# A second Strassen level for one of the seven half products of W2, with some evictions moved to ScalarE and new instruction lists

## The chip, the core and the metric

The kernel runs on one core of a Trainium2 chip, with one launch. The metric is the device time of that core in microseconds. Before the change it is 2509.16 us, the median of three runs (2508.62 to 2509.91). The engines are TensorE (PE in the profile; PEld is its loading of weights), VectorE (DVE), ScalarE (ACT), GpSimd (POOL) and SyncE (SP), which here only issues DMAs.

## What is computed

The input x is 128 graphs of 128 nodes with 256 features, in fp32; adj is 128 x 128. Four layers follow each other, each on h = max(layernorm(x), 0) and each added to x:

```python
# layer 0: gated sums over neighbours
x = x + relu((A_in h + eb) * sig(h g0) + (A_out h + oeb) * sig(h g1) + h * sig(h g2))
# layer 1: causal attention with adj as mask, weights Wqkv, Wo
x = x + softmax(q k^T / 16 + adj, causal) v @ Wo
# layer 2: three graph convolutions, weighting = adj * adj
h = relu(weighting (h W1)); h = relu(weighting (h W2)); x = x + weighting (h W3)
# layer 3: A_hat h, then Linear(256,512), batchnorm over all rows, relu, Linear(512,256), batchnorm
x = x + layer3(h)
```

W1 is 256 x 512, W2 512 x 1024, W3 1024 x 256. The batch statistics of layer 3 go over all 128 x 128 rows, so that layer is done in three passes: up to its first product, its second product, and the output.

## The kernel before

The 128 graphs are 32 groups (NG) of four; a group is T = 512 rows. The first pass takes a group through layers 0, 1 and 2 and the first product of layer 3, written z to DRAM. The change touches the first pass alone.

Big products are done by `seven` (L535), the Winograd form of Strassen's algorithm with one level: both operands are cut into quarters, and seven half-size products take the place of eight. Products 0, 5, 6 and 3 add up in one PSUM bank (px), 4 and 2 in another (pz), and product 1 has a bank of its own (py). In between ScalarE copies px or pz to a tile named kept (L542), and `put` lets VectorE add such a copy to a bank. The sums of quarters of the data are made by `sums` (L490 to L496), those of the weights once by `weight_sums` (L236).

`layer2` (L862) does W2 as two calls of `seven` (`wide(0)` and `wide(1)`; each takes 256 of the 512 columns of a half product), then W3. In `wide` each of the seven products is eight records of TensorE: 2 output chunks x 2 chunks of the contraction, 256 rows wide, each matmul leaving two records. The add of product 1 is at L885, and a relu by ScalarE follows (L887). `us` holds the quarters and sums of the activations u after mixing with the adjacency (uT).

`mixed` (L468) multiplies by an adjacency matrix: four 128 x 128 matmuls into one bank, then an eviction. The engines that evict are a tuple, used in turn; for uT (L857) and gT (L968) it held VectorE alone, for mT (layer 1) VectorE and ScalarE.

All these are Python generators that yield after each step. Which stream makes its next step is written out by hand in strings: HEAD for the first groups, TURN once for each of groups 1 to 29, and TAIL for the last two. In TURN a letter stands for a stream: A is layer 0 of group g + 2, B layer 1 of group g + 1 (b that of g + 2), C layer 2 of group g, D layer 3 of group g - 1 (d that of g). `in_turn` then ties the instructions of each engine, and DMA issues of POOL and SP, to this order, so that every engine works through its own queue in exactly the order of the letters.

Of the kernel before, what the change touches and what calls it, by code (L numbers as in the profile page):

```python
# [8 lines left out]
FP = mybir.dt.float32  # L9
AF = mybir.ActivationFunctionType  # L10
# [5 lines left out]
P = 128  # L16
# [6 lines left out]
def kernel(  # L23
# [58 lines left out]
    def bank(shape, name):  # L82
        return psum[-1].tile(shape, FP, tag="bank", name=name)
# [31 lines left out]
    ZT = {}  # L115

    weights = passA.enter_context(tc.tile_pool(name="weights", bufs=1))
    adj_sb = weights.tile([P, P], FP, name="adj_sb")
    nc.scalar.dma_start(adj_sb, adj)
    xin = passA.enter_context(tc.tile_pool(name="xin", bufs=4))  # L120
    X = {}
# [15 lines left out]
    gw = weights.tile([P, 3, D], FP, name="gw")  # L137
    gb = weights.tile([P, 3], FP, name="gb")
    nhalf = const.tile([P, 8], FP, name="nhalf")
    adjT = weights.tile([P, P], FP, name="adjT")  # L140
    ain = weights.tile([P, P], FP, name="ain")
    aout = weights.tile([P, P], FP, name="aout")
    maskb = weights.tile([P, P], FP, name="maskb")
# [7 lines left out]

    stats1 = weights.tile([P, FC, NG + 2, 6], FP, name="stats1")
    stats2 = const.tile([P, DC, NG + 1, 6], FP, name="stats2")
    bw1T_12 = weights.tile([P, F1 // 2], FP, name="bw1T_12")

    nc.gpsimd.memset(nhalf, -0.5)
    nc.gpsimd.memset(gb, 0.0)
# [34 lines left out]
    table = const.tile([P, 1], FP, name="table")  # L192
    nc.scalar.activation(table, nhalf[:, 0:1], AF.Exp)

    vrow = small.tile([NV, P], FP, name="vrow", bufs=1)
    deg = small.tile([P, 4], FP, name="deg", bufs=1)
    dinv = small.tile([P, 1], FP, name="dinv", bufs=1)

# [28 lines left out]
    def set_of(b, extra):  # L227
        b11, b21, b12, b22 = quarters(b)
        return b11, b21, b22, extra[:, 2], extra[:, 0], extra[:, 1], b12

    SETS = {}
    for k, b in ("2", w2), ("1", w1), ("3", w3), ("q", m_qk), ("v", w_vo), ("b", bw1T):
        _, nk, nf = b.shape
        SETS[k] = set_of(b, weights.tile([P, 3, nk // 2, nf // 2], FP, name=f"set_{k}"))

    def weight_sums(operands):  # L236

        b11, b21, b22, t4n, t1, t2, b12 = operands
        nc.vector.tensor_tensor(t1, b12, b11, ALU.subtract)
        yield  # L240
        nc.vector.tensor_tensor(t2, b22, t1, ALU.subtract)
        yield
        nc.vector.tensor_tensor(t4n, b21, t2, ALU.subtract)
        yield
        nc.vector.tensor_tensor(b12, b22, b12, ALU.subtract)
        yield

    BW2T = scratch.tile([P, FC, D], FP, name="BW2T")
    BW2S = scratch.tile([P, 3, FC // 2, D // 2], FP, name="BW2S")
    bw2s = bw1[:, :3, :].rearrange("p a (b c) -> p a b c", b=FC // 2)  # L250

# [13 lines left out]
    def warming():  # L265

        for n in FILL:
            awake(n)
            yield

    def gate_rows():

        for i, v in enumerate((gate_weight, out_gate_weight, loop_gate)):
            nc.sync.dma_start(
                gw[:, i, :], bass.AP(tensor=v.tensor, offset=v.offset, ap=[[0, P], [1, D]])
            )
        yield
# [76 lines left out]
    def last_weights():  # L354

        yield from turned(bw1T, bw1, FC, "bw1T")
        yield from turned(bw2t, bw2, DC, "bw2T")
        yield from weight_sums(set_of(bw2t, bw2s))
        nc.sync.dma_start(BW2S, bw2s)
        nc.sync.dma_start(BW2T, bw2t)  # L360
        yield
        pv = bank([P, NV], "pv")
        nc.tensor.transpose(pv, vrow, ident[:NV, :NV])
        yield
        nc.vector.tensor_copy(vecs, pv)
        yield
        nc.scalar.copy(bw1T_12, bw1T[:, 0, F1 // 2 :])
        yield
        yield from weight_sums(SETS["b"])

# [128 lines left out]
    def quarters_t(aT):  # L499

        return quarters(aT)
# [30 lines left out]

        return product

    def seven(product, put, shape, name, pool=None):  # L535

        def kept(pb, i):  # L540
            t = (pool or w).tile(shape, FP, tag="kept", name=f"{name}_t{i}", bufs=6)
            nc.scalar.copy(t, pb)  # L542
            return t

        px = bank(shape, f"{name}_x")
        product(0, px, True)
        yield SPLIT
        t1 = kept(px, 1)
        yield
        py = bank(shape, f"{name}_y")  # L550
        product(1, py, True)
        yield SPLIT
        yield from put((0, 0), py, t1)
        yield
        pz = bank(shape, f"{name}_z")
        product(4, pz, True)
        yield SPLIT
        t5 = kept(pz, 5)
        yield
        product(5, px, False)  # L560
        yield SPLIT
        t2 = kept(px, 2)
        yield
        product(2, pz, False)
        yield SPLIT
        yield from put((0, 1), pz, t2)
        yield
        product(6, px, False)
        yield SPLIT
        yield from put((1, 1), px, t5)  # L570
        yield
        product(3, px, False)
        yield SPLIT
        yield from put((1, 0), px, None)
        yield
# [105 lines left out]
    def layer1(g, bs=ALL):  # L681
# [172 lines left out]
        uT = tile_of(g, bs, [P, HC1, T], "uT", f"uT_{g}", 1)  # L854
        ex = tile_of(g, bs, [P, 3, HC1 // 2, T // 2], "us", f"us_{g}", 1)
        US[g] = summed(quarters_t(uT), ex)
        yield from mixed(uT, u, a2T, f"pmu_{tail}", (nc.vector.tensor_copy,), bs)  # L857
        if bs[-1] == G - 1:
            yield from sums(nc.vector, quarters_t(uT), ex)
        yield  # L860

    def layer2(g):  # L862

        us = US[g]
        h2T = w.tile([P, HC2, T], FP, tag="h2T", name=f"h2T_{g}", bufs=1)

        a11, a12, a21, a22 = quarters_t(h2T)
        ex = w.tile([P, 3, HC2 // 2, T // 2], FP, tag="h2s", name=f"h2s_{g}", bufs=1)
        h2s = (a11, a12, ex[:, 2], a22, ex[:, 0], ex[:, 1], a21)

        def wide(q):
            def put(ij, pb, other):
                i, j = ij
                j = j * HC2 // 2 + 2 * q
                dst = h2T[:, j : j + 2, i * T // 2 : (i + 1) * T // 2]
                if other is None:
                    nc.scalar.activation(dst, pb, AF.Relu)
                    mine = slice(2 * q, 2 * q + 2)
                    yield SPLIT
                    yield from sums(  # L880
                        nc.vector,
                        [a[:, mine] for a in (a11, a12, a21, a22)], ex[:, :, mine],
                    )
                else:
                    nc.vector.tensor_tensor(dst, pb, other, ALU.add)  # L885
                    yield SPLIT
                    nc.scalar.activation(dst, dst, AF.Relu)  # L887

            return seven(
                columns_by_half(us, SETS["2"], 2 * q), put, [P, 2, T // 2], f"p2_{g}_{q}"  # L890
            )

        S = []
# [57 lines left out]
    def layer3(g):  # L951
# [13 lines left out]
            yield  # L965
        gT = tile_of(g, parts[0], [P, DC, T], "dT", f"gT_{g}", 2)
        for i, bs in enumerate(parts):
            yield from mixed(gT, h, ahT, f"pg_{g}_{i}", (nc.vector.tensor_copy,), bs)  # L968
            if g < LAST:
                ex = w.tile([P, 3, 1, T // 2], FP, tag="ex", name=f"gs_{g}", bufs=2)  # L970
                gs = yield from sums(nc.vector, quarters_t(gT), ex)
            yield
# [29 lines left out]
        for i, j in (0, 0), (1, 0), (0, 1), (1, 1):  # L1002
            pb = bank([P, 2, T // 2], f"pz_{g}_{i}_{j}")
            for jj in range(2):
                for c in range(DC):
                    at = (2 * j + jj) * P
                    b = bw1T_12[:, jj * P : (jj + 1) * P] if (c, j) == (0, 1) else bw1T[:, c, at : at + P]
                    nc.tensor.matmul(
                        pb[:, jj, :], b, gT[:, c, i * T // 2 : (i + 1) * T // 2],
                        start=(jj == 0 and c == 0), stop=(c == DC - 1), skip_group_check=True,  # L1010
                    )
            yield from put((i, j), pb, None)
            yield

    def bn_part(stats, nch, groups, name):
# [7 lines left out]


    TURN = (
        "ACCCBCCCCCAADBDBBBCDDCDDCCDDABBBBBAADCCBBCBCDBBAADABDCBBABBCCCCCCAAACCCD"
        "CCCAADDDDAADCDDCCCDBBCCAADBBCDBBBBBBBBCCCCAAAAADDDBBbCCCCCCCbbBBBBBCCbbB"
        "BDDBBDBBBBBBBBCCBCCBBBCCCCBBBDBDDDDDDDBBBBBBBBbBBBBdbb"
    )
    BEGUN = 8  # L1030
    PINNED = tuple(
        getattr(mybir.EngineType, e) for e in ("PE", "DVE", "Activation", "Pool", "SP")
    )
    TAIL = (
        "CCCCCCCCCBBBBBDDDDDDBBBBBDDDCBBBCCCBBDDBBCCCBBCCCCCCBBCCCCCCCCCCCCBCDDBB"
        "BBBBBBBCCCBCCCCCCCCCBBBBBBBBBCCCBBBBDBBBBDDBDDDBCBCBBBBBCBDCCDDBBBBCCBBB"
        "BBBEBEEEEEEBBEEEEEEDDDFDEEEEEEFFFFFFFEEEEFDDEEEEDDDDEEEFFEEEEEDFDDEEEEDE"
        "EDEEEEEEESEEEEFEEFFEFFFEEFEEFGEFFGGFFFFFGFFFFGGGGGGGGGFFGFGGGGSE"
    )
    US, MIX = {}, {}  # L1040
    AHEAD = 3
# [14 lines left out]
    def part(f, g):  # L1056
# [4 lines left out]
    HALVES = range(G // 2), range(G // 2, G)  # L1061
    FILL = (5, 28, 6, 8, 9, 2, 4)
    HEAD = (
        "wiiwiaaaapppppcciiipmaaappwammaccccacaeeppppppccaccwaaceewaacapppppccbbw"
        "eeecppecwbbbbebddeeAembbbbbededdddbbbeeeogdbbbmbeedddbeooommdboooooobbbo"
        "bpdddemedbbbeddbedfffoobbbbbbpppdopdbbbbbbbbdCfffffdddfAAffnCCfffffffffA"
        "ddddfofpofoAddddndpAAfffddddddddfdffddCddfCCCCCCffnnACCCCfCoAACCACAACCCC"
        "CCCCCCCAAnnnnnAfCCCCCCoffffffAffffCCCCCCACCACCCCfffnCfAAAAABBBffffffffnC"
        "ConBfBffffoofCCCfCffffooCCfffCCCCCDDDffffffffffffBfBB"
    )  # L1070
    load_x(AHEAD)
    ds, bs = layer3(0), layer1(2)
# [2 lines left out]
        "b": layer1(0, HALVES[0]), "d": layer1(0, HALVES[1]),  # L1075
        "e": layer0(1), "f": layer1(1), "A": layer0(2), "B": bs, "C": layer2(0), "D": ds,
        "i": gate_weights(), "p": attention_weights(), "m": mixing_weights(), "n": network_weights(),
        "o": last_weights(), "w": warming(), "g": gate_rows(),
    }
    for k in HEAD:  # L1080
        at = len(nc.cur_bb.bb.instructions)
        next(stream[k], None)
        in_turn(at, PINNED)
    at = len(nc.cur_bb.bb.instructions)
    for k in "abcdefACipmnowg":
        for _ in stream[k]:
            pass
    assert len(nc.cur_bb.bb.instructions) == at
# [293 lines left out]
```

## Time and profile before

| | |
|---|---|
| median of three runs | 2509.16 us |
| the profiled execution | 2508.19 us |
| its span | 2506.4 us |
| granted TensorE clock | 0.997 |
| busy: PE / DVE / ACT / POOL | 2476.3 / 2006.6 / 1161.3 / 314.4 us |
| main loop, groups 1 to 29 | a turn of 68.73 us each |
| second pass and output | from about 2240 us on |

The profile is of one execution. Its lines of groups have the source line, engine, operation, output <- inputs by the names of tiles, shapes, and then busy time, mean duration in ns, and the idle time of the engine before them with what ended it. In the timeline the first number is the start in us from the span's start, the second the time from the first start to the last end of the merged instructions. Lines of waits have the sum in us, the number of times and the longest. Lines of a stretch have its length and then each engine's busy time in it.

### The profile page before, as it was taken

To read this page: it belongs to the slowest core of one execution; us is meant where nothing else is said; L and a number is where in the kernel's file an instruction comes from. 1 tells how busy PE (TensorE), PEld (TensorE's weight loads), DVE (VectorE), ACT (ScalarE), POOL (GpSimd) and SP (SyncE) were. 2 spreads that over 40 slices of the span, in tenths; PEclk is the share of its full clock that TensorE was granted. 3 is DMA by queue.
4 is the path that set the end of the run, shared out by engine and by line. 5 is a ranking of instruction groups with operands and counts; after the bars stand their busy time and mean duration, and the time that the engine had idled before them with its cause. 6 is when DMAs were issued, how large, how long until landed. Compare 5 with 4: busy or idle time off the path is not lost. (4 is left out here: it accounts for less than half of the span.)

```text
span 2506.4 us, 37984 instructions
## 1 busy us (share of the span) xinstructions
PE 2476.3 (99%) x13232; PEld 2189.2 (87%) x13232; DVE 2006.6 (80%) x4891; ACT 1161.3 (46%) x2486; POOL 314.4 (13%) x563
## 2 busy tenths in 40 slices
PE   9999999999999999999999999999999999999996
PEld 7888888888888888888888888888888888888885
DVE  7878887888888788887888887888878887568886
ACT  5344444444434444444444444444444444337767
POOL 2111111111111111110111111111101111000000
PEclk9999999999999999999999999999999999999998
DMA  4112222222222222222222222222222222145459
GB/s 153 43 51 76 73 79 85 85 76 76 76 79 82 64 72 77 76 84 85 78 74 78 83 77 64 74 79 72 85 85 80 76 72 76 26 158 210 170 198 388
DMA packets 136771, 237.83 MB, mean 95 GB/s; under 512 B 13938, under 2 KB 94852, under 8 KB 132612
## 3 DMA queue, kind: packets, MB, share of 16 engines
q1 hardware_dynamic: 130148, 212.79, 27.7%
q0 software_dynamic: 6288, 22.55, 2.5%
q8 instruction: 105, 1.72, 0.3%
q14 instruction: 86, 0.70, 0.1%
q10 hardware_dynamic: 144, 0.07, 0.0%
HBM read 120.93 MB, written 114.43 MB: 94 GB/s over the span
## 5 line engine op out<-in xcount | busy, mean ns | idle before, releaser
L423 ACT ACTIVATE h<-x,sh,rs 128x256 f32<-128x256 f32 x512 | 268.8, 590 | 109.6 <-POOL sh L409 99.4
L887 ACT ACTIVATE h2T<-h2T 128x512 f32<-128x512 f32 x192 | 120.8, 629 | 370.7 <-DVE h2T L885 370.7
L406 POOL TENSOR_SCALAR rs<-mv 128x4 f32<-128x4 f32 x124 | 36.1, 291 | 1751.9 <-DVE mv L402 1723.1
L527 PE MATMUL p_x<-uT,w 128*128 128x256 f32 x1024 | 242.2, 379 | 0.0
L527 PEld LDWEIGHTS p_x<-uT,w 128*128 128x128 f32 x1024 | 187.5, 190 | 22.3 <-issue 0.2
L398 DVE BATCH_NORM_STATS2 st<-x 128x6 f32<-128x256 f32 x512 | 187.0, 413 | 1.1
L542 ACT COPY p_t<-p_x 128x512 f32<-128x512 f32 (+1 forms) x192 | 97.3, 507 | 166.0 <-PE p_x L527 159.0
L605 DVE SCALAR_TENSOR_TENSOR gs<-h,gw 128x256 f32<-128x256 f32 x360 | 152.4, 423 | 15.1 <-ACT h L423 0.6
L407 POOL TENSOR_TENSOR rs<-rs,nhalf 128x4 f32<-128x4 f32 x124 | 142.2, 1147 | 10.3
L527 PE MATMUL p_x<-uT,set 128*128 128x256 f32 x512 | 121.1, 379 | 0.6 <-DVE h2T L885 0.6
L473 PEld LDWEIGHTS pmu<-a2T,u 128*128 128x128 f32 x1024 | 119.4, 192 | 2.1 <-PE pr L942 0.2
L527 PE MATMUL p_z<-us,w 128*128 128x256 f32 x512 | 121.1, 379 | 0.0
L527 PE MATMUL p_z<-us,set 128*128 128x256 f32 x512 | 121.0, 379 | 0.0
L527 PE MATMUL p_y<-uT,w 128*128 128x256 f32 x512 | 121.0, 379 | 0.0
L527 PE MATMUL p_x<-us,set 128*128 128x256 f32 x512 | 121.0, 379 | 0.0
L473 PE MATMUL pmu<-a2T,u 128*128 128x128 f32 x1024 | 119.7, 275 | 0.0
L527 PEld LDWEIGHTS p_z<-us,w 128*128 128x128 f32 x512 | 97.1, 190 | 25.2 <-issue 6.9
L836 ACT ACTIVATE u<-u 128x512 f32<-128x512 f32 x93 | 58.6, 630 | 127.0 <-DVE u L834 127.0
L917 PE MATMUL p_x<-h2T,w 128*128 128x256 f32 x480 | 113.4, 379 | 0.0
L994 DVE BATCH_NORM_STATS2 stats<-zo 128x6 f32<-128x512 f32 x120 | 77.3, 685 | 44.2 <-ACT zo L988 43.2
L527 PEld LDWEIGHTS p_x<-us,set 128*128 128x128 f32 x512 | 97.3, 190 | 13.2
L527 PEld LDWEIGHTS p_y<-uT,w 128*128 128x128 f32 x512 | 97.2, 190 | 13.2
(346 smaller groups left out, 5977.1 us busy)
## 6 DMA issues: line engine op xcount, KB each, us to landing
z<-zo SPq DMA_DIRECT2D x62, 512.0 KB, 5.3
zi<-z SPq DMA_DIRECT2D x31, 1024.0 KB, 4.9
x<-x POOLq DMA_DIRECT2D x32, 512.0 KB, 3.4
x<-in_x_dram SPq DMA_DIRECT2D x31, 512.0 KB, 3.8
hc<-h SPq DMA_DIRECT2D x120, 128.0 KB, 2.4
h<-hc SPq DMA_DIRECT2D x30, 512.0 KB, 3.5
sc<-s SPq DMA_DIRECT2D x120, 128.0 KB, 2.4
s<-sc SPq DMA_DIRECT2D x30, 512.0 KB, 4.2
```

Source lines behind the costliest of these rows:

```text
L398: nc.vector.bn_stats(st[:, k, :], xt[:, b, :])
L406: nc.gpsimd.tensor_scalar(rs, mv[:, :, 1], LN_EPS, None, ALU.add)
L407: nc.gpsimd.tensor_tensor(rs, rs, nhalf[:, :n], ALU.pow)
L423: nc.scalar.activation(dst, src, AF.Relu, bias=sh[:, k : k + 1], scale=rs[:, k : k + 1])
L473: nc.tensor.matmul(pm[:, k, :], src[:, b, c * P : (c + 1) * P], aT, start=True, stop=True)
L527: nc.tensor.matmul(pb[:, jj, :], b_r[r][:, c, at : at + P], a_r[r][:, c, :], start=(first and jj == 0 and c == 0), stop=(c == nk - 1), ski ...
L542: nc.scalar.copy(t, pb)
L605: nc.vector.scalar_tensor_tensor(gs, h[:, b, :], 1.0, gw[:, i, :], ALU.mult, ALU.mult, accum_out=gl[:, k, i : i + 1],)
L836: nc.scalar.activation(dst, dst, AF.Relu)
L887: nc.scalar.activation(dst, dst, AF.Relu)
L917: nc.tensor.matmul(pb, SETS["3"][r][:, c, :], h2s[r][:, c, :], start=(first and c == 0), stop=(c == HC2 // 2 - 1), skip_group_check=True,)
L994: nc.vector.bn_stats(stats1[:, 2 * j + jj, g, :], z[j][:, jj, :])
```

## The change

1. In `layer2`, for all groups but the first, product 1 of W2 (a12 by b21, 256 rows x 256 x 256 in each call) is no longer done as one product but by Strassen's algorithm again (`leaf`): seven products of 128 x 128 x 128, each one matmul. They alternate between two banks of their own (lx, ly), and VectorE adds the partial results onto the kept t1 or into h2T. `leaf_rows` makes four sums of quarters of a12 on VectorE, once for both calls. `leaf_sums` makes the weights' sums once, in HEAD (stream q).
2. The evictions of uT and gT alternate between VectorE and ScalarE.
3. The kept tiles have five buffers where they had six. The tile bw1T_12 is gone: its columns are written to DRAM in HEAD and read back on SP's queue into the tile of gs when layer 2 of the last group begins. adj_sb, adjT and vrow share the tiles of the leaf's weight sums.
4. HEAD, TURN and TAIL are new strings (TURN 222 letters for 198; the 24 more are all C).

```diff
-    def seven(product, put, shape, name, pool=None):
+    def seven(product, put, shape, name, pool=None, whole=True):
...
-            t = (pool or w).tile(shape, FP, tag="kept", name=f"{name}_t{i}", bufs=6)
+            t = (pool or w).tile(shape, FP, tag="kept", name=f"{name}_t{i}", bufs=5)
...
-        py = bank(shape, f"{name}_y")
-        product(1, py, True)
-        yield SPLIT
+        py = None
+        if whole:
+            py = bank(shape, f"{name}_y")
+            product(1, py, True)
+            yield SPLIT
         yield from put((0, 0), py, t1)
...
-        yield from mixed(uT, u, a2T, f"pmu_{tail}", (nc.vector.tensor_copy,), bs)
+        yield from mixed(uT, u, a2T, f"pmu_{tail}", (nc.vector.tensor_copy, nc.scalar.copy), bs)
...
+    def leaf_rows(a, extra):
+
+        a11, a12, a21, a22 = quarters_t(a)
+        s1, s2, s4, s3 = (e.rearrange("p (k t) -> p k t", k=1) for e in extra)
+        for out, one, two in (s1, a21, a22), (s2, s1, a11), (s4, a12, s2), (s3, a11, a21):
+            nc.vector.tensor_tensor(out, one, two, ALU.add if out is s1 else ALU.subtract)
+            yield SPLIT
+        return a11, a12, s4, a22, s1, s2, s3
+
+    def leaf(a_r, b_r, dst, t, name):
+
+        def product(pb, r, first):
+            nc.tensor.matmul(
+                pb, b_r[r][:, 0, :], a_r[r][:, 0, :], start=first, stop=True,
+                skip_group_check=True,
+            )
...
+        def onto(i, j, pb):
+            mine = part_ij(t, i, j)
+            nc.vector.tensor_tensor(mine, pb, mine, ALU.add)
+
+        def put(i, j, pb):
+            nc.vector.tensor_tensor(part_ij(dst, i, j), pb, part_ij(t, i, j), ALU.add)
+
+        px = bank([P, P], f"{name}_lx")
+        product(px, 0, True)
+        yield SPLIT
+        onto(0, 0, px)
+        yield SPLIT
+        py = bank([P, 2, P], f"{name}_ly")
+        product(py[:, 1], 4, True)
+        product(py[:, 0], 1, False)
+        yield SPLIT
+        onto(1, 1, py[:, 1])
+        yield SPLIT
+        product(px, 5, False)
+        yield SPLIT
+        onto(0, 1, px)
+        yield SPLIT
+        product(py[:, 1], 2, False)
+        yield SPLIT
+        nc.vector.tensor_tensor(dst[:, :, :P], py, t[:, :, :P], ALU.add)
+        yield SPLIT
+        product(px, 6, False)
+        yield SPLIT
+        put(1, 1, px)
+        yield SPLIT
+        product(px, 3, False)
+        yield SPLIT
+        put(1, 0, px)
+        yield SPLIT
...
+                if pb is None:
+                    if not leaf_a:
+                        spare = ex[:, 0, 2:, :].rearrange("p k (h t) -> p (k h) t", h=2)
+                        leaf_a.append(
+                            (yield from leaf_rows(us[1], [spare[:, k] for k in range(4)]))
+                        )
+                    yield from leaf(leaf_a[0], leaf_set(q), dst, other, f"p2_{g}_{q}")
+                    nc.scalar.activation(dst, dst, AF.Relu)
...
-                columns_by_half(us, SETS["2"], 2 * q), put, [P, 2, T // 2], f"p2_{g}_{q}"
+                columns_by_half(us, SETS["2"], 2 * q), put, [P, 2, T // 2], f"p2_{g}_{q}",
+                whole=(g == 0),
...
-            yield from mixed(gT, h, ahT, f"pg_{g}_{i}", (nc.vector.tensor_copy,), bs)
+            yield from mixed(gT, h, ahT, f"pg_{g}_{i}", (nc.vector.tensor_copy, nc.scalar.copy), bs)
```

Below, a product of the leaf is named by its number: l0 to l6; o00, o11 and o01 are its three adds onto t1 in the order of the code.

## The prediction, made before the changed kernel was run

> **What bounds the kernel now.** I read the page's busy shares and slices first, then one steady turn of the main loop as a stretch, then TensorE in order of time, then the waits.
>
> ```profile
> PE 2476.3 (99%) x13232; PEld 2189.2 (87%) x13232; DVE 2006.6 (80%) x4891; ACT 1161.3 (46%) x2486; POOL 314.4 (13%) x563
> PE   9999999999999999999999999999999999999996
> DVE  7878887888888788887888887888878887568886
> 1357.44:1426.17 68.73, 68.73 (x368) 60.99 (x367) 56.05 (x141) 30.24 (x67) 9.60 (x17) 1.00 0.28 77
> ```
>
> The last line is one turn (us, then busy PE, PEld, DVE, ACT, POOL, clock, DMA share). TensorE is busy for all of it; VectorE for 56.05 of 68.73 us (82%), ScalarE for 30.24. A busy PE need not run at its pace, so look at the starts:
>
> ```profile
> 1353.98 3.73 PE L473 MATMUL pmu<-a2T,u 128*128 128x128 f32 x32
> 1357.55 1.89 PE L527 MATMUL p_x<-uT,w 128*128 128x256 f32 x8
> 1359.28 1.89 PE L527 MATMUL p_y<-uT,w 128*128 128x256 f32 x8
> ...
> 1422.71 3.73 PE L473 MATMUL pmu<-a2T,u 128*128 128x128 f32 x32
> ```
>
> One matmul of the program leaves two records. 32 records of 128 columns take 1357.55 - 1353.98 = 3.57 us, **112 ns each**; eight of 256 take 1359.28 - 1357.55 = 1.73 us, **216 ns each**; two of 512 take 0.86 us in the timeline, 430 each. A turn issues 108, 254 and 4 of them (counted from the stages): 108 x 0.112 + 254 x 0.216 + 4 x 0.430 = 68.68 us. The turn from one pmu to the next is 1422.71 - 1353.98 = 68.73 us. So TensorE loses 0.05 us in a turn: pace, not waiting, sets the main loop. The one wait that costs is small:
>
> ```profile
> PEld py L805 <- issue: 7.4, 28, 0.3
> DVE s L912 <- PE p_z L917: 77.7, 28, 2.8
> ```
>
> (28 turns.) The py wait ends when VectorE's transpose of p lands; between the rows before and after it, about 0.13 us of TensorE are lost. VectorE on the other hand waits for TensorE, some 12 us in a turn.
>
> [...]
>
> ```profile
> L885 DVE TENSOR_TENSOR h2T<-p_y,p_t 128x512 f32<-128x512 f32 x64 | 43.7, 683 | 1.4 <-PE p_y L527 1.4
> L912 DVE TENSOR_TENSOR s<-p_y,p_t 128x256 f32<-128x256 f32 x32 | 13.5, 423 | 13.9 <-ACT p_t L542 13.7
> L243 DVE TENSOR_TENSOR set_v<-w_vo,set_v 128x128 f32<-128x128 f32 x1 | 0.3, 285 | 0.0
> L477 DVE COPY uT<-pmu 128x512 f32<-128x512 f32 (+1 forms) x132 | 79.7, 662 | 0.8 <-PE pmu L473 0.6
> ```
>
> **The change, part by part, for one group.**
>
> *TensorE.* The second half product of W2 (r = 1 in seven) is two times eight records of 256 columns: 16 x 0.216 = 3.46 us. In its place stand two times seven products of one matmul, 28 records of 128 columns: 28 x 0.112 = 3.14 us. Saved: **0.32 us**. It applies to groups 1 to 31 (whole stays for group 0): 31 x 0.32 = 9.9 us; with unrounded paces (111.6 ns, 216) 0.33 and 10.3 us. I take 10.3.
>
> *VectorE.* Away: two adds of 512 columns (2 x 0.683) and three evictions that go to ScalarE (two of uT, one of gT: 3 x 0.66): 3.35 us. New: four sums on a12, and in each half five adds of 128 columns and one of 256: 14 x 0.285 + 2 x 0.424 = 4.84 us. Net +1.5 us: 57.5 of 68.4 us, 84%. ScalarE gets 3 x 0.58 = 1.7 us: 32 of 68.4. Neither becomes a bound by its total. What hides the 1.5 us is VectorE's 12 us of waiting for TensorE, if the list puts it there.
>
> *The new waits.* A leaf's products return to the same two banks (px, py): product l5 needs the first add out of px, l2 the one out of py, l6 and l3 the next out of px. Behind a waiting product all of TensorE's queue stands. I laid the new TURN out letter by letter (A 24, B and b 79, C 81, D and d 38 steps: C has 24 more). Between l5 and its add's product lie 6 us of other matmuls in the first leaf; the tightest is l2 of the first leaf, whose add (o11) stands at the end of a long VectorE queue that begins at the previous turn's last pz adds. There are 24 VectorE instructions from the (1, 1) add of pz to o11. How long they take is read from the timeline:
>
> ```profile
> 1358.39 1.23 DVE L463 STREAM_TRANSPOSE hT<-h 128x1024 f32<-128x1024 f32 x1
> 1359.55 0.65 DVE L490 TENSOR_TENSOR us<-uT 128x512 f32<-128x512 f32 x1
> 1360.23 0.69 DVE L492 TENSOR_TENSOR us<-us,uT 128x512 f32<-128x512 f32 x1
> ...
> 1361.57 0.68 DVE L496 TENSOR_TENSOR uT<-uT 128x512 f32<-128x512 f32 x1
> 1362.17 1.24 DVE L463 STREAM_TRANSPOSE s<-s 128x1024 f32<-128x1024 f32 x1
> ```
>
> An instruction that doesn't depend on the one before starts about 0.07 us before that one's end (1359.55 against 1358.39 + 1.23 = 1359.62; 1362.17 against 1362.25). By these start-to-start times the 24 take 13.4 us, and they begin 0.2 us after their product's slot and hand over 0.1 us after their end: 13.7. TensorE has 5.3 us of matmuls to the turn's end and 8.7 in the next turn before l2: 14.0. So l2 is met with **0.3 us to spare**. In the same way l5 has 0.6, l6 0.3, l3 0.1; in the second leaf l5 0.5, l2 0.6, l6 0.6, l3 0.3. By whole durations, without overlap, the 24 would take 14.8 and l2 would be 1.0 us late. The trace shows the overlap in every turn, so I take no stall; 1.0 is kept as the upper end. A gain below nothing is excluded: no product can run ahead of TensorE's order.
>
> *Buffers.* kept goes from 6 to 5: by the layout at most four are alive at once (pz's t5 stays longest), so ScalarE's copies find one free. Cost zero; if not, a copy waits for a put, under 0.7 us of an engine that is idle half the time. Banks: p2 px, pqv px, pqv pz, pr1, lx, ly are the most at once, six of eight.
>
> *Head and tail.* leaf_sums: four VectorE adds of 256 columns once, 1.7 us, against some 3 us of evictions that leave VectorE there. One ScalarE copy goes; one 128 KB write and, in the last group, one 128 KB read on SP's queue come: the layout has tens of us between the read's issue and its use, and transfers of 128 KB land in 2.4 us by the page's DMA rows[...]. The new HEAD and TAIL are taken at zero, with 2 us either way: by stretches TensorE is idle for 4.0 of the first 66 us and 0.6 of the next 55, which a new order can shift. In the tail two leaf groups are among the 31. The output phase is unchanged.
>
> *Sum.* The profiled execution took 2508.2 us (span 2506.4), 1.0 under the median of 2509.16. 2508.2 - 10.3 = 2497.9 for it; against the median 2509.2 - 10.3 = **2499**.
>
> **The rivals.**
>
> *Slower: VectorE late at the leaf (0.10).* If the leaf's adds don't overlap (they are short, and two of four sums depend on the one before), l2 is 1.0 us late in each turn: 31 x (1.0 - 0.33) = +21, **2530**. It decides from 0.33 us of stall in a turn. For it: VectorE at 84%, slacks of 0.1 to 0.6 us. Against: VectorE's starts overlap in all rows that don't depend, and the list of before loses only 0.05 us at 82%.
>
> *Half given back (0.10).* Slacks of 0.1 and 0.3 us fail in part: one wait missed costs about what py's costs, 0.13; with one or two in a turn 0.2 is lost, 31 x 0.13 = 4 are gained: **2505**, half of it above the 0.2% mark.
>
> *Pairs don't keep 112 ns (0.07).* The gain is nil at 16 x 216 / 28 = 123 ns a record. pmu, pg and ps run in rows of eight and more; pairs of 128 between matmuls of 256 are in no row here (pqv has rows of four, which keep 110). At 120 the gain is 31 x 0.1 = 3: **2506**.
>
> *Head or tail gain (0.08).* The new lists take 3 us out of the head's losses as well: **2496**.
>
> **How the numbers follow.** The forecast, 0.65: 2497 to 2502. About 0.2% (5 us) can be told from no change here. Faster by more: 0.65 + 0.08 + half of 0.10 = 0.78. Within: 0.05 + 0.07 = 0.12. Slower: 0.10. The range goes from the head's gain, 2495, to the pairs' and half cases, 2507; it leaves out the slow rival and the edges.
>
> **What would show it.** Right: the turn from pmu to pmu at 68.4 us, 374 records, leaf records 112 ns apart, VectorE near 57.5 us in a turn. The slow rival would show as PEld waiting for the leaf's adds (l2, l3 first) and a turn over 68.7. Pairs at fault: starts over 120 ns apart with no wait named. Wrong in the lists: a head to the first steady turn that is longer or shorter by over 2 us.

## The result, and the profile after

The changed kernel takes **2500.62 us** (median of seven runs, 2499.95 to 2501.45). The kernel before, beside it on the same chip, takes 2508.74 us (2508.01 to 2509.91). The ratio is 0.9967, with a 95% interval of 0.9956 to 0.9979: 8.1 us less, where 10.3 were forecast. The profiled execution of the changed kernel took 2501.45 us, span 2499.6.

The page of the changed kernel, its busy shares and two rows of its slices:

```profile
PE 2469.3 (99%) x13604; PEld 2192.4 (88%) x13604; DVE 2021.5 (81%) x5230; ACT 1256.3 (50%) x2584; POOL 289.0 (12%) x563
...
PE   9999999999999999999999999999999999999996
...
DVE  7878888888888888888888888888888887568886
```

TensorE is still busy throughout, with 372 more records (12 in each of 31 groups). One turn as a stretch (columns as before: us; busy PE, PEld, DVE, ACT, POOL; clock, DMA share, GB/s):

```profile
1356.00:1424.50 68.50, 68.50 (x380) 61.05 (x379) 56.56 (x152) 33.34 (x70) 8.73 (x17) 1.00 0.27 78
```

VectorE and ScalarE have room left, 12 and 35 us. So the question is again how long a turn is. From pmu to pmu:

```profile
1348.63 3.73 PE L486 MATMUL pmu<-a2T,u 128*128 128x128 f32 x32
1352.20 1.89 PE L540 MATMUL p_x<-uT,w 128*128 128x256 f32 x8
...
1417.14 3.73 PE L486 MATMUL pmu<-a2T,u 128*128 128x128 f32 x32
```

1417.14 - 1348.63 = **68.51 us**; the first four turns of the loop have 68.46. What a turn takes without any gap between its records was measured further down: **68.60 us** with the old products (number 7) and **68.27** with the new ones (number 12). I call **lost** what a matmul starts later than the pace of the record before it (112, 216, 430 ns). The old turn of 68.73 lost 0.13, at py; the new one loses 0.19 and, from the fifth turn, 0.24. By place, py's loss is gone, and pu's and pg's have come. The waits of the changed kernel in the 28 turns from 188 to 2113 us (total us, times, longest):

```profile
PEld pqv_z L725 <- issue: 13.9, 58, 0.2
...
PEld pu_x L523 <- DVE u L849: 9.0, 28, 0.3
...
PEld pg L486 <- ACT h L436: 0.2, 1, 0.2
```

The first line costs nothing: weight loads that idle while matmuls still run (pqv_z starts at 1357.63, 1.72 us after pr's start at 1355.91: pr's four records of 430 ns). In the second one the load waits 0.32 us per turn, and TensorE loses 0.19 us there. It is none of the leaf's products: pu is W1's product, which the change doesn't touch. The timeline of the changed kernel at that place:

```profile
1344.99 1.03 PE L523 MATMUL pu_x<-w,mT 128*128 128x256 f32 x4
1345.85 1.03 PE L540 MATMUL pz_x<-gT,bw1T 128*128 128x256 f32 x4
1346.80 1.13 PE L523 MATMUL pu_x<-set,mT 128*128 128x256 f32 x4
1347.77 1.03 PE L540 MATMUL pz_x<-gT,set_b 128*128 128x256 f32 x4
```

```profile
1346.80 0.73 PEld L523 LDWEIGHTS pu_x<-set,mT 128*128 128x128 f32 x4 [0.32 <-DVE u L849]
```

```profile
1346.06 0.69 DVE L849 TENSOR_TENSOR u<-pu_x,pu_t 128x512 f32<-128x512 f32 x1
1346.92 0.69 DVE L1064 TENSOR_TENSOR zo<-pz_x,pz_t 128x512 f32<-128x512 f32 x1 [0.17 <-PE pz_x L540]
```

The second row of TensorE starts 0.86 us after the first, as paced; the third 0.95 after the second, and the fourth 0.97 after the third. Product 6 of `seven` goes into bank px, VectorE adds it up (put (1, 1)), and product 3 goes into the same bank, so it may not start before the add has read it. From the end of product 6's slot (1345.85) to the start of the add (1346.06) there are 0.21 us, the add takes 0.69, and the next product begins 0.05 after its end: a **round trip** of 0.95 in these rows. The record behind the one that waited also comes late, by 0.10 us (0.97 for 0.86, rounded): 1.05 in all. The load that waited begins at 1346.80 together with its matmul, while the load of the first row begins at 1344.78, 0.21 us ahead of its matmul; that this makes the 0.10 fits, but no run tests it. Only one product, 0.86 us, stands between. In the new TURN the last products are pu.r2, pu.r6, pz.r6, pu.r3, pz.r3 (r is the product's number).

In the kernel before, the same pair was covered. Its TensorE has W3's last product, 1.72 us, between pu.r6 (first row) and pu.r3 (third row), and nothing is lost there:

```profile
1349.66 1.03 PE L510 MATMUL pu_x<-w,mT 128*128 128x256 f32 x4
1350.53 1.89 PE L917 MATMUL p_x<-h2T,set 128*128 128x256 f32 x8
1352.25 1.03 PE L510 MATMUL pu_x<-set,mT 128*128 128x256 f32 x4
```

The new list took that product away from there and put one of half its length in its place.

### The profile page after: what moved, and what is told of

It is laid out like the page before. It is cut to its first block, busy times and chain, and to the rows that moved or that the text cites. A ratio compares the mean times of both kernels' runs of the same rounds, so it can differ in the third digit from the quotient of the medians.

```text
span 2499.6 us, 39001 instructions
## 1 busy us (share of the span) xinstructions
PE 2469.3 (99%) x13604; PEld 2192.4 (88%) x13604; DVE 2021.5 (81%) x5230; ACT 1256.3 (50%) x2584; POOL 289.0 (12%) x563
## 4 chain that ended last, share of the span: by engine, by line
PE 95%; ACT 2%; DVE 1%; issue 0%; POOL 0%; ACTq 0%; DVEq 0%; POOLq 0%
PE p_x L540 17%; PE p_z L540 9%; PE p_x L1001 8%; PE pmu L486 5%; PE pu_x L523 5%; PE po_x L1331 4%; PE pz_x L540 4%; PE p_z L1001 4%; PE pg L486 2%; PE pm L486 2%; PE po_z L1331 2%; PE py L820 2%; PE pr L1026 2%; PE p_lx L889 2%; PE pqv_x L730 2%; PE pm L684 2%
## 5 line engine op out<-in xcount | busy, mean ns | idle before, releaser
L411 DVE BATCH_NORM_STATS2 st<-x 128x6 f32<-128x256 f32 x512 | 179.4, 411 | 0.1
L420 POOL TENSOR_TENSOR rs<-rs,nhalf 128x4 f32<-128x4 f32 x124 | 136.0, 1097 | 10.3
L849 DVE TENSOR_TENSOR u<-pu_z,pu_t 128x512 f32<-128x512 f32 x31 | 21.4, 692 | 117.6 <-PE pu_z L523 117.6
L970 ACT ACTIVATE h2T<-h2T 128x512 f32<-128x512 f32 x130 | 78.2, 623 | 60.4 <-DVE h2T L968 60.4
L540 PEld LDWEIGHTS p_x<-uT,set 128*128 128x128 f32 x512 | 94.7, 190 | 11.8 <-DVE h2T L968 0.3
L1001 PEld LDWEIGHTS p_x<-h2T,w 128*128 128x128 f32 x480 | 91.1, 190 | 12.3
L540 PEld LDWEIGHTS p_z<-us,set 128*128 128x128 f32 x512 | 92.5, 190 | 10.1
```

The source lines that it names most:

```text
L411: nc.vector.bn_stats(st[:, k, :], xt[:, b, :])
L420: nc.gpsimd.tensor_tensor(rs, rs, nhalf[:, :n], ALU.pow)
L540: nc.tensor.matmul(pb[:, jj, :], b_r[r][:, c, at : at + P], a_r[r][:, c, :], start=(first and jj == 0 and c == 0), stop=(c == nk - 1), ski ...
L1001: nc.tensor.matmul(pb, SETS["3"][r][:, c, :], h2s[r][:, c, :], start=(first and c == 0), stop=(c == HC2 // 2 - 1), skip_group_check=True,)
```

## Experiments

A time in the text below is a median; the kernel before stood at 2508.6 to 2509.1 in every comparison. Losses per turn are read from starts, as above.

### Where the wait comes from

**1. W3's last product moved into the gap.** Two letters of TURN move behind pu.r6 (CC behind BBBBB), one d by one letter.

```diff
-"...bBbBBBDCBBBBBCCCBBBBBDDDCBBDD..." "dBBbBb"
+"...bBbBBBDCBBBBBCBBBBBCCDDDCBBDD..." "BdBbBb"
```

> The changed kernel with two letters of C (W3's product r3 and its copy) moved behind pu's product r6, so that 2.6 us of matmuls instead of 0.9 stand between pu.r6 and pu.r3; d goes one letter later, behind the second sum of us. Theory: the missing part of the gain is the wait of pu.r3 for its add, 0.19 us in each turn, and it comes from the place in the list alone. Then a turn goes from 68.51 to 68.3 us and the time to 2500.6 - 29 x 0.19 = 2495. Rival: the wait is VectorE's new load and turns up elsewhere, or the swap of s, now 1.7 us later, makes VectorE's transpose late: the turn stays at 68.5 and the time at 2500 to 2502.

Measured 2506.11 us, ratio 0.999 (0.9982 to 0.9998): 5.5 us slower than the changed kernel. The waits of this kernel:

```profile
PEld pz_x L540 <- DVE zo L1064: 9.0, 28, 0.3
PEld pu_z L523 <- ACT pu_t L555: 7.5, 28, 0.3
```

The old wait is gone, and the same one has come up at pz: pz.r6 and pz.r3 now have only pu.r3's 0.86 between them, and lose the same 0.187. pu.r2 follows its copy too closely (0.134), since W3's product no longer stands ahead of it. In six turns pr, which needs the later swap of s, loses up to 0.48 us besides, 1.7 us in all. The theory's time was wrong: a pair may not be mended alone. That the pair decides, and not VectorE's load, is still what fits: the loss is 0.187 at either place.

**2. Without the leaf.** All of the change stays but the leaf: product 1 is done as one product in every group, the leaf's other letters do nothing, and of its four weight sums the last, which overwrites a block of the weights, is left out.

```diff
-                if pb is None:
-                    if not leaf_a:
...
-                elif other is None:
+                if other is None:
...
-                whole=(g == 0),
+                whole=4 * (g > 0 and q == 0),
```

> The changed kernel with its lists and evictions, but with product 1 of W2 whole again, at the letter of the leaf's first product; its add stands at the letter of the leaf's add of two quarters, the other letters of the leaf issue nothing. Theory: the leaf saves 0.33 us a group and the wait of pu.r3 is not its doing, so it stays: 2500.6 + 31 x 0.33 = 2511, the turn 68.84, pu.r3 still waiting 0.19. Rival: the 1.5 us of VectorE's new work make that wait; without them it goes and the time is 2505. Second rival: the new lists brought the gain, and the time stays near 2501.

Measured 2513.80, ratio 1.002 (1.0011 to 1.0028). pu.r3 still loses 0.188 in each turn, so this wait belongs to the new list and not to the leaf. The turn is 68.90, 0.39 more than with the leaf: 0.33 by the pace, 0.10 by a wait of pqv_z that appears where the leaf's products stood, less 0.05 at pg. In these lists the leaf is worth 13 us, 10 of them by its own products. Its stretch also gives the leaf's load on VectorE:

```profile
1300.00:1368.90 68.90, 68.90 (x368) 60.99 (x367) 54.38 (x138) 33.16 (x70) 8.64 (x17) 1.00 0.26 77
```

**3. No cover at all.** pz.r6 and its add go behind pu.r3 (the DDD of TURN moves by three letters).

```diff
-"...CBBBBBCCCBBBBBDDDCBBDDBb..."
+"...CBBBBBCCCBBBBBCBBDDDDDBb..."
```

> The changed kernel with pz.r6 and its add behind pu.r3 instead of before it: nothing stands between pu.r6 and pu.r3. Theory: the whole round trip shows, about 1.05 us instead of 0.19 in each turn, 2500.6 + 29 x 0.86 = 2525. Rival: the wait is not of this pair but of VectorE's queue as a whole, which also has less ahead of it now: under 0.5 us a turn, below 2510.

Measured 2555.70, ratio 1.0184 (1.017 to 1.0198):

```profile
PEld pz_x L540 <- DVE zo L1064: 32.0, 27, 1.2
PEld pu_x L523 <- DVE u L849: 32.0, 27, 1.2
```

I had counted one pair, but pz.r6 and pz.r3 have become neighbours too. Each of the two loses **1.05 us** in every turn. So the round trip with nothing between is 1.05, and with 0.86 between it 1.05 - 0.86 = 0.19: the loss in the changed kernel, to the hundredth.

### Evictions on ScalarE

**4. The changed kernel with the evictions back on VectorE.**

```diff
-f"pmu_{tail}", (nc.vector.tensor_copy, nc.scalar.copy), bs)
+f"pmu_{tail}", (nc.vector.tensor_copy,), bs)
...
-f"pg_{g}_{i}", (nc.vector.tensor_copy, nc.scalar.copy), bs)
+f"pg_{g}_{i}", (nc.vector.tensor_copy,), bs)
```

> The changed kernel with all evictions of uT and gT on VectorE again, lists unchanged. Theory: the leaf's waits have 0.3 to 0.6 us to spare, and two more evictions (1.2 us) in VectorE's queue ahead of the leaf's adds use that up: l4, l5 or l2 are late by 0.6 to 0.9 us in a turn, 2500.6 + 31 x 0.75 = 2524. Rival: VectorE idles 12 us in a turn and absorbs 1.9 us: 2501 to 2503.

Measured 2525.39, ratio 1.0067 (1.0053 to 1.0081): 24.8 us more than with ScalarE's share. The turn is 69.35 or a little less, with 0.30 lost at pr, 0.20 to 0.36 at the leaf's l2, 0.18 at the leaf's products 4 and 1, and pu's 0.19. So VectorE late at the leaf, which the slow rival of the forecast feared, lies near, though here it comes from more work in the queue and not from adds that fail to overlap. What kept it away are three evictions per turn; how much of that is uT's and how much gT's was not tried in these lists.

**5. The kernel before with both evictions shared**, nothing else (the reverse of that diff).

> The kernel before with the evictions of uT and gT shared with ScalarE, lists unchanged. Theory: TensorE keeps its pace there with 0.05 us of loss in a turn, so relief of VectorE brings nothing: 2508 to 2509.5, the turn 68.7. Rival: the relief is a gain of its own: 2 us or more less.

Measured 2523.97, ratio 1.0061 (1.0045 to 1.0076). I had not expected 15 us more. py's loss rises from 0.13 to 0.65 per turn. Timelines of this kernel, of ScalarE and of VectorE:

```profile
1397.13 0.63 ACT L887 ACTIVATE h2T<-h2T 128x512 f32<-128x512 f32 x1 [1.18 <-DVE h2T L885]
1397.66 0.57 ACT L542 COPY p_t<-p_z 128x512 f32<-128x512 f32 x1
1398.13 0.91 ACT L643 ACTIVATE m<-eb,gt 128x256 f32<-128x256 f32 x2
1398.94 0.57 ACT L477 COPY gT<-pg 128x512 f32<-128x512 f32 x1
```

```profile
1399.54 0.42 DVE L490 TENSOR_TENSOR gs<-gT 128x256 f32<-128x256 f32 x1 [1.15 <-ACT gT L477]
...
1402.62 0.68 DVE L463 STREAM_TRANSPOSE p<-pT 128x512 f32<-128x512 f32 x1
```

gT's second product starts at 1393.34 (8 x 112 ns: through by 1394.3), but its copy begins at 1398.94. ScalarE is idle a good part of the time (in the kernel before it was busy for 30.24 of a turn's 68.73 us), and the copy still stands in it behind a relu that waits for VectorE, a copy and two bias copies. VectorE, which has to sum gT next, idles for 1.15 us, and the transposition of p, which py waits for, stands behind that.

**6. The same for uT alone.**

> The kernel before with only the evictions of uT shared with ScalarE, those of gT left on VectorE. Theory: the 15 us that both together cost come from gT's second eviction, which stands behind four copies of layer 0 in ScalarE's queue, so that VectorE waits 1.15 us for it and p's transpose and py are late; uT's alone costs nothing: 2508 to 2510. Rival: ScalarE is late for exp because of uT: 2515 or more.

Measured 2509.12, ratio 1.0002 (0.9994 to 1.001), py at 0.12: all of the 15 us come from gT's eviction, and uT's gives nothing here.

**7. Number 5 with gT's product and copy issued a few letters earlier**, ahead of that relu.

```diff
-"...BBCCCCCCAAACCCD" "CCCAADDDDAADCDD..."
+"...BBCCCCCCAAACDDC" "CCCCAADDDAADCDD..."
```

> before_scalar_evict with the second product of pg and its eviction on ScalarE issued a few letters earlier: on TensorE nothing changes place, on ScalarE the copy goes ahead of a relu of h2T, a copy of p_z and two bias copies (m<-eb). In before_scalar_evict pg's matmuls ended near 1394.5 us and the copy began at 1398.9, while the first sum of gT idled VectorE for 1.15 us. Theory (the 15 us are this place in ScalarE's queue and nothing else): the copy begins within 1.7 us of its product, VectorE's idle time there goes, the transposition of p is no later than before, py waits no more than before (0.13 us in a turn), and the time is the kernel before's, 2508.8 us, or up to 3.5 us less as VectorE has 2 us less to do in each turn. Rival (ScalarE's share as such costs, wherever it stands): py still waits 0.4 us or more, and the time stays above 2516 us.

Measured 2505.11, ratio 0.9985 (0.9978 to 0.9992). Timeline of ScalarE in this kernel (the matmuls of gT's second product begin at 1381.70 in it):

```profile
1384.21 0.56 ACT L477 COPY gT<-pg 128x512 f32<-128x512 f32 x1
```

py's loss is zero, the turn 68.60. The eviction's place in ScalarE's queue is worth 19 us (2523.97 - 2505.11). Well placed, the shared evictions gain 4 us without any leaf, which is py's loss, 0.13 x 29 = 3.8 us.

### Toward a version without losses

**8. Three places at once.** pz.r6 goes ahead of pu.r2, W3's last product behind pu.r6, the transposition of s (d) behind us.s4, pr0 and pr1 behind pqv's product 4.

```diff
-"CCCBCCCCBBBCDDDBBBCBCCC..." "...CBBBBBCCCBBBBBDDDCBBDDBb..." "dBBbBb"
+"CCCBCCCCBBBCBBDDDBCBCCC..." "...CBBBBBCDBDBBBBCBCCDDBDBb..." "BBdbBb"
```

> The changed kernel with TURN laid anew by hand at three places: pz.r6 moves ahead of pu.r2, W3's r3 behind pu.r6, so that at least 1.7 us of matmuls stand between each pair that shares a bank (pu r5 and r6, pu r6 and r3, pz r6 and r3); the transpose of s goes behind the third sum of us, and the two products pr behind pqv's r4, because the swap of s now starts 2.6 us later. Theory: what is missing of the gain is the round trip of about 1.05 us (0.2 to the add, 0.69 for it, 0.05 and a bare weight load back) against 0.86 of cover, so a turn goes from 68.51 to 68.3 us and the time to 2500.6 - 29 x 0.19 = 2495. Rival: the late swap takes it back at pr or in the leaf: 2500 or more.

Measured 2502.80, ratio 0.9977 (0.9968 to 0.9986). In most turns all three waits are gone (68.32, pg's 0.05 left). But the swap of s through DRAM starts 2.6 us later, and in several of the loop's first ten turns it comes too late; timeline of such a turn:

```profile
323.37 0.34 SPq L472 DMA_DIRECT2D s<-sc  x1
329.31 1.25 DVE L476 STREAM_TRANSPOSE s<-s 128x1024 f32<-128x1024 f32 x1 [1.98 <-DMA s<-sc]
330.61 0.70 PE L1026 MATMUL pr<-s,a2T 128*128 128x512 f32 x1 [1.50 <-DVE s L476]
```

The read is issued at 323.37, and VectorE waits for it until 329.31, 5.9 us after the issue; the median landing of this read is 4.1 in the DMA rows of the changed kernel. These turns lose up to 1.95 us at pr, 6.8 us in all, and the tail another 1.3: the rival, a late swap that takes the gain back, came true. Why the read lands late in these turns was not traced.

**9. The same, and layer 3's second pair of relus ahead of the W2 copy on ScalarE** (in TURN, "CCCCCABDBB" becomes "CCCCDCABBB").

> The same, and the second half of layer 3's relus goes ahead of one relu of h2T in ScalarE's queue, so that pg no longer waits for it (0.05 us a turn). Theory: 1.5 us under the run before, 2493.5. Rival: the relu of h2T, now 1 us later, makes the sums of h2s late, and nothing is gained.

Measured 2501.06, ratio 0.9968 (0.9956 to 0.9981). Steady turns are 68.27, and pg's wait is gone. The late swaps stay, 6.8 us in the first ten turns and 1.2 in the tail.

**10. The transposition of s taken into the next turn**, and the leaf's products 4, 1 and 5 ahead of pr0 and pr1; TAIL is laid in the same way. The diff is against number 9.

```diff
-"CCCBCCCCBBBCBBDDDBCBCCCBBCCCCBBC..." "BBdbBb"
+"CCCBCCCCBBCDBCCCCBBBBDDDBCCBCCBBC..." "BBBbBb"
...
-    ds = after(8, ds)
+    ds = after(9, ds)
```

> The order of both_covered_relu, and the start of the turn laid anew so that the swap of s has more time: the transposition of s goes from the end of one turn into the next (behind the leaf's first sum on VectorE), and its two products pr0 and pr1 stand behind the leaf's products 4, 1 and 5 and behind products 4 and 5 of q and v on TensorE, 1.55 us later than in both_covered (0.45 + 0.22 + 0.88). The tail is laid the same way. Theory (what both_covered_relu still lost, 6.1 us in turns 2 to 10 and 1.2 in the tail, was the late swap alone): pr waits at most 0.4 us in any turn, steady turns stay at 68.3, and the time is 2501.1 - 6.1 - 1.2 = 2493.8 us, with 2492.5 to 2496 taken as a hit. Rival (the start of the turn has no room for it): VectorE stands in its queue for pr1 ahead of q's first put, so the leaf's last products (p_lx of product 3, slack 0.1 us in my lay-out) or product 2 wait 0.2 to 0.5 us in every turn, the turn becomes 68.5 to 68.8, and the time is 2500 to 2508 us.

Measured 2545.49, ratio 1.0147 (1.0132 to 1.0163). The swap is never late, as the theory had it, but every turn takes 70.01; start of a turn on TensorE:

```profile
1311.97 0.61 PE L730 MATMUL pqv_y<-w_vo,hT 128*128 128x128 f32 x4
1313.29 0.46 PE L889 MATMUL p_ly<-h2s,leaf 128*128 128x128 f32 x2 [0.71 <-DVE h2s L882]
1313.59 0.39 PE L889 MATMUL p_ly<-uT,w 128*128 128x128 f32 x2
1314.47 0.49 PE L889 MATMUL p_lx<-h2s,leaf 128*128 128x128 f32 x2 [0.49 <-DVE p_t L899]
```

I had moved the leaf's product 4 ahead by 2.6 us (to 3.7 us after the turn's first product, from 6.3, counted without the loss) without asking when its operand is there: the first sum of the leaf stands in VectorE's queue behind the sums of uT and hT and ends at 1313.14 (0.95 lost). The first add out of lx stands behind the leaf's other sums (0.76). The rival had the leaf and VectorE's queue, but named other products (3 or 2) and pr1 as what stands ahead, and put the loss at 0.2 to 0.5 us where it is 1.7.

**11. The relus alone**, on the changed kernel: the edit of number 9 and nothing else.

> The changed kernel with one letter of the turn moved: the second pair of relus of layer 3 is issued ahead of the eviction of W2's wide product behind it on ScalarE. Theory (pg's wait for this relu, 0.05 us in each turn from turn 5 on, is the rest of the loss that the evictions on ScalarE brought): the wait goes and nothing else moves, 24 x 0.05 = 1.2 us, 2499.4 us, pu's wait of 0.19 stays. Rival: the eviction that is passed is itself met with little to spare, W2's next product waits for it, and the time is the changed kernel's 2500.6 or up to 2 us more.

Measured **2498.68**, ratio 0.996 (0.9948 to 0.9973), 68.46 in every turn, no wait at pg. Expected were 2499.4.

**12. Number 11 with product 6 ahead of product 2 in pu.** Its order is now 6, 2, 3; pz.r6 and its add (two letters D) stand between 6 and 2, and the relu of part (0, 1) follows that of (1, 0).

```diff
+        rest = ((2, pz, (0, 1), t2), (6, px, (1, 1), t5))
+        for r, pb, ij, t in rest[::-1] if six_first else rest:
+            product(r, pb, False)
+            yield SPLIT
+            yield from put(ij, pb, t)
+            yield
...
             if other is None:
                 nc.scalar.activation(dst, pb, AF.Relu)
+                nc.scalar.activation(late[0], late[0], AF.Relu)
...
-"...BBBBBCCCBBBBBDDDCBB..."
+"...BBBBBCCCBBBDDBBDCBB..."
```

> relu_first with the last products of u (pu) in the order 6, 2, 3 in place of 2, 6, 3, the last product of z (pz.r6) between 6 and 2, and the relu of put (0,1) behind the one of put (1,0) on ScalarE. So pz.r6 and pu.r2 (1.72 us) lie between pu.r6 and pu.r3, which overwrites the bank that VectorE's add reads, and pu.r2 and pu.r3 (1.72 us) lie between pz.r6 and pz.r3; W3's last product, and with it the swap of s, stays where it is. The round trip was 1.05 us. Theory (the 0.19 us of a turn is the pair with 0.86 us of cover, and nothing else is near): the wait goes, turn 68.46 - 0.19 = 68.27, time 2498.7 - 29 x 0.19 = 2493.2 us, with 2492 to 2495 taken as a hit. Rival (the wait turns up elsewhere, as with W3's product moved): pmu waits for the relus at the end of u, or the swap, or pu.r6 for ScalarE's copy, 0.1 to 0.2 us in a turn, and the time is 2496 to 2500 us.

Measured **2494.22** (2492.28 to 2494.88), ratio 0.9941 (0.9927 to 0.9954): 14.6 us under the kernel before and 6.4 under the changed one. The same place as above, on TensorE of this kernel:

```profile
1338.61 1.02 PE L523 MATMUL pu_x<-w,mT 128*128 128x256 f32 x4
1339.47 1.03 PE L540 MATMUL pz_x<-gT,bw1T 128*128 128x256 f32 x4
1340.33 1.03 PE L523 MATMUL pu_z<-w,ms 128*128 128x256 f32 x4
1341.20 1.03 PE L523 MATMUL pu_x<-set,mT 128*128 128x256 f32 x4
1342.06 1.03 PE L540 MATMUL pz_x<-gT,set_b 128*128 128x256 f32 x4
1342.92 0.27 PE L486 MATMUL pmu<-a2T,u 128*128 128x128 f32 x1
```

Every row starts 0.86 or 0.87 after the one before. Both pairs have two products between them, W3's product and the swap behind it stay where they were, and all turns of the loop take 68.27 us: nothing is lost any more.

## Why the forecast was right, and where it was not

**TensorE paces the loop, and a leaf saves 0.32 to 0.33 us.** Right. Turns without a gap take 68.60 and 68.27. The 0.05 us that TensorE was said to lose in a turn came from rounded paces, which sum to 68.68; against the 68.60 it is the 0.13 of py's wait. The forecast counted 374 records in the new turn; that was a slip, 366 + 12 are 378.

**Single pairs of 128 columns keep the pace.** Right, and the rival of 120 ns is out. Timeline of the changed kernel, one leaf in the tail:

```profile
2168.95 0.38 PE L889 MATMUL p_ly<-h2s,leaf 128*128 128x128 f32 x2
2169.17 0.39 PE L889 MATMUL p_ly<-uT,w 128*128 128x128 f32 x2
2169.40 0.39 PE L889 MATMUL p_lx<-h2s,leaf 128*128 128x128 f32 x2
2169.63 1.56 PE L1001 MATMUL p_x<-h2T,set 128*128 128x256 f32 x6
```

Two records take 0.22 to 0.23 us, 110 to 115 ns each, also ahead of a product of 256 columns. In the loop l0, l5 and l3 of the first leaf stand alone between other products, and the starts behind all 756 records of the leaves in 27 turns come 109 to 112 ns later. (The record of a load lasts 186 to 192 ns in this loop and overlaps the next, and 112 ns are kept all the same.)

**The leaf's own waits are met.** Right. The overlap of independent VectorE instructions carried over to the short adds: the second row below starts 0.05 us before the first one ends. In the changed kernel, the add that l2 waits for (o11, first row), and l2 itself:

```profile
1360.02 0.28 DVE L899 TENSOR_TENSOR p_t<-p_ly,p_t 128x128 f32<-128x128 f32 x1
1360.25 0.29 DVE L899 TENSOR_TENSOR p_t<-p_lx,p_t 128x128 f32<-128x128 f32 x1
```

```profile
1360.93 0.39 PE L889 MATMUL p_ly<-h2s,w 128*128 128x128 f32 x2
```

o11 ends at 1360.30; with 0.05 to hand over, 0.58 us are to spare, 0.3 were forecast. VectorE takes 13.38 us from the start of pz's (1, 1) add (1346.92, shown above) to the end of o11, as forecast (13.4); of the spare time, 0.19 is pu.r3's own loss, which puts l2 off as well. (Without overlap l2 would have been 1.1 us late by the forecast's own terms, not 1.0: 0.2 + 14.8 + 0.1 - 14.0.) l2 starts 8.73 us into the turn; by hand it was 8.7. No product of the leaf loses time in any turn of the loop.

**"So I take no stall": the step that failed.** The sum 10.3 - 0 took in the leaf's waits alone. But all lists were laid anew, and the pairs of the other products had to be laid out in the same way. pu.r6 and pu.r3 were in the layout with one product between, and the forecast's own terms for the leaf, 0.2 us to the add's start, 0.69 for the add, 0.1 to hand over, make 0.99 against the 0.86 of that product. In the kernel before, 1.72 us had stood there. The mis-sized term is the loss of a turn: held as it was (0.13), measured 0.19 to 0.24. pu's 0.19 in 29 turns are +5.5, pg's 0.05 in 24 are +1.2, and py's 3.8 come back, which the forecast had not counted as a gain: -10.3 + 5.5 + 1.2 - 3.8 = -7.4, where -8.1 were measured. By the two profiled executions everything ahead of layer 3's second product (first row of po at 2243.97 and 2236.20) became 7.8 us shorter. The difference of 0.7 is no more than lies between single runs of the changed kernel (1.5 us), so nothing is read from it.

That the forecast came so close is in part luck. 6.7 us were lost and 3.8 gained that it had not counted; without py's 3.8 the time would have been 2504.4, outside 2497 to 2502.

Number 12 is without pu's and pg's terms: 2508.8 - 10.3 - 3.8 = 2494.7 by this sum, 2494.2 measured.

**Evictions on ScalarE: 1.7 us of an idle engine.** The amount was right as a count (three copies of 0.573), the meaning wrong. They are not filling: without them the new lists lose 24.8 us, and in the old lists they cost 15 us or gain 4, by their place in the queue. ScalarE's busy time rose by 3.1 us in a turn; three copies make 1.7. By whole durations its instructions take 1.85 us more in a turn (34.86 to 36.71), so the rest of the 3.1 is less overlap in time.

**VectorE, +1.5 us per turn.** Too high: 56.05 to 56.56 in busy time. From number 2, the leaf brings 56.56 - 54.38 = 2.2 (3.5 by whole durations), and the evictions take away 1.7 (2.0). Busy time counts an overlap once: by whole durations VectorE's instructions take 63.73 us in the turn before and 65.18 in the new one, 1.45 more where busy time has 0.51. An estimate from the forecast's 0.07 us of overlap for each of 14 more short instructions is 1 us.

**Buffers.** Number 12 has five kept tiles and loses nothing in the loop, so the sixth was not needed: cost zero, right.

**Head and tail.** The first steady boundary came 0.8 us earlier (p_x behind pmu at 188.51 and 187.73), 0.3 of it a leaf; the stretch of the last groups is 0.3 us shorter, where two leaves save 0.66. Zero, with 2 us either way, holds.

**The rivals.** "Half given back" was close: it put 0.2 us of loss in a turn, and 0.19 to 0.24 were measured, but at pu and pg and not at the leaf. Only py's 3.8 us, which it did not count either, kept the net loss at a quarter of the gain. The slow rival did not come about; number 4 shows how near it was.

## What to carry to other kernels

When a list of instructions is laid anew, lay out **every** pair of a bank's reader and its next writer, not only the new ones: here a pair lost its round trip less what stood between, 1.05 - 0.86 in the changed kernel and all of the 1.05 in number 3. When such a pair is mended, ask what leaves its old place (number 1: another pair; number 8: a swap that starts 2.6 us later). And an idle engine takes work in its queue's order (number 5: gT's copy began 4.6 us after its product, and the time rose by 15 us): ask what its queue waits for ahead of the moved instruction, and who waits behind.

## What was not expected of the hardware

The round trip from TensorE over a VectorE add of 128x512 back to TensorE was 1.05 us (number 3), of which the add was 0.69 in the changed kernel's rows and the lateness of the record behind the one that waited 0.10. TensorE ran a hand-laid queue of 378 records a turn with no gap at all in number 12: 68.27 us in each of 28 turns. The swap's read of 512 KB landed after 4.1 us in the median of the changed kernel; in three early turns of number 8 VectorE could use it only 5.5 to 6.1 us after its issue.
